# Cross-attention on one core: the energies by three float32r passes over halves of gx and y in place of Strassen's seven float32 products, and the values made with positions on the partitions

## The chip, the cores and the metric

The kernel runs on one core of a Trainium2 chip. The metric is the device time of one launch in microseconds, taken from runs of the whole program; the profile is one further look at one execution, with the start and the end of every instruction on TensorE (its weight loads as a row of their own, PEld), VectorE (DVE), ScalarE (ACT), GpSimd (POOL) and SyncE (SP).

## The reference

There are 32 batches; in each, `x` and the context `y` have 256 channels and 1024 positions, in float32. What is computed for a batch:

```python
x_q = einsum('oc,bcn->bno', w_qk, y)
x_k = einsum('oc,bcn->bon', w_qk, x)
x_v = einsum('oc,bcn->bon', w_v, x) + b_v
energy = einsum('bnc,bcm->bnm', x_q, x_k)          # 1024 x 1024
attention = softmax(energy, axis=-1)
attention = attention / (1e-07 + attention.sum(axis=1, keepdims=True))
x_r = einsum('bcn,bnm->bcm', x_v, attention)
out = x + relu(einsum('oc,bcn->bon', w_t, x - x_r) + b_t)
```

The kernel folds the weights once: gx is x under w_qk's own product (with the sign turned), so that an energy is y times gx over 256 channels; "values" are x under the product of w_t and w_v (with the sign turned), so that the attention product gives the output's channels at once.

## The kernel before

Everything is float32. A 256 x 1024 operand is seen as four quadrants of 128 partitions x 512 columns, and each of the four products of a batch (gx, values, energies, attention) is made by Strassen's scheme in the form with seven products (class `Seven`, line 252): products p1, p5, p2, p6, p3, p7, p4, of which several are added onto one another in the same PSUM bank, and four combinations c11, c12, c22, c21. The scheme keeps three banks: p6 is added onto p1's bank, ScalarE then copies that bank to SBUF (`kept`, tag `w`), and only then p7 and p4 may be added onto it; c11 reads p2's bank and the copy of p1. A product takes factors that are sums of quadrants: for x these (`xs`) are made by accumulating DMAs on GpSimd's queue (lines 225 to 250), for y (`ys`) in the same way, for gx (`gt`, line 324) and the values (`us`, line 384) by four GpSimd operations of 512 columns each.

For each batch b, in the loop at line 664:

- **Energies** (class `Energy`, lines 402 to 455). For each of four steps t, seven products of 128 x 512 give the four quadrants of two rows of tiles (rows t and t + 4, each 128 x 1024). ScalarE evicts three partial sums; VectorE combines each quadrant with one custom instruction that also keeps the running minimum (or, for the rows t + 4, the maximum) and is followed by a small read of that accumulator (`nm`). ScalarE takes the exponential of a row of 1024 (`exp`) and its sum (`rs`), VectorE takes the reciprocal (`ri`) and adds the scaled row to `acc` (`share`); one row in eight is scaled by ScalarE. The combination c21 reads a constant tile `zeros`.
- After the first step t = 0, the last product of the batch before (`before.end()`, five products) and its combination c21 with the store are made.
- **gx of batch b + 1** (class `Keys`), then most of the **values of b + 1** (class `Values`). The values come out with channels on the partitions and are needed with positions on the partitions: `turn` (line 367) makes four VectorE transposes of 32 x 32 blocks, and `move` (line 375) sixteen copies of 32 partitions x 512, split between VectorE (8 a batch) and ScalarE (8 a batch), or DMAs in the first and the last batch. The bias of the values is added on ScalarE.
- `columns` and `inverse` (lines 597 and 611) sum `acc` over the partitions and take the reciprocals `rc`.
- **Attention** (class `Attention`, lines 457 to 595). `normal` scales the rows of `e` by both reciprocals (16 VectorE operations of 512), `mix` makes the sums of their quadrants (eight of 1024, tiles `et` for t1, t2 and t4), and each of the seven products is five TensorE products: one of x (`xpart`) and four over tiles of `e` (`epart`). The results are combined with relu and x and stored.

Every compute engine's instructions run in the order in which the program issues them: the class `InOrder` (line 66) chains each instruction of TensorE, VectorE, ScalarE and GpSimd to the one before it on the same engine:

```python
behind = nullcontext() if self.last is None else tc.issue_after(self.last.ins)
with behind:
    self.last = getattr(self.engine, name)(*args, **kwargs)
```

So an instruction that waits holds up all that stands behind it on its engine. SyncE's DMAs are placed by the framework. All matrix results use one pool of eight PSUM banks of 512 columns, taken in rotation (line 64); evictions and combinations go through a pool of two buffers a tag (`temp`, line 219). All TensorE, VectorE, ScalarE and GpSimd instructions carry line 77 in the profile, since `InOrder` issues them; they are told apart by their tiles: `pg` gx, `pu` values, `pe` energies, `po` attention.

Of the kernel before, what the change touches and what calls it, by code (L numbers as in the profile page):

```python
# [9 lines left out]
F32 = mybir.dt.float32  # L10
AF = mybir.ActivationFunctionType
ALU = mybir.AluOpType
# [4 lines left out]
def kernel(  # L17
# [22 lines left out]

# [12 lines left out]
    BIG = 3.0e38  # L59

    const = ctx.enter_context(tc.tile_pool(name="const", bufs=1))
    xp = ctx.enter_context(tc.tile_pool(name="xp", bufs=2))
    yp = ctx.enter_context(tc.tile_pool(name="yp", bufs=1))
# [25 lines left out]
    def load(tag, b, pieces=1):  # L89
        from_, p = (x, xp) if tag == "x" else (y, yp)  # L90
        to = p.tile([P, KC, N], F32, tag=tag, name=f"{tag}_{b}")
        from_ = from_[b].rearrange("(k p) n -> p k n", p=P)
        W = KC // pieces
        for j in range(pieces):
            nc.sync.dma_start(to[:, ts(j, W)], from_[:, ts(j, W)])
        loaded[tag, b] = to
# [18 lines left out]
    scratch = ep.tile([P, 3, HT, MB], F32, tag="et", name="scratch").rearrange(  # L115
# [8 lines left out]
    bv = scratch[:, 4, :KC].rearrange("p (k o) -> p k o", o=1)  # L124
    bt = const.tile([P, KC, 1], F32, name="bt")
    nbt = const.tile([P, KC, 1], F32, name="nbt")
    bu = const.tile([P, KC, 1], F32, name="bu")
    nbu = const.tile([P, KC, 1], F32, name="nbu")
    for k, start in enumerate((nc.sync.dma_start, act.dma_start)):
        start(wqk[:, k], w_qk[ts(k, P)])  # L130
    load("x", 0, KC)
# [4 lines left out]
    load("y", 0)  # L136


    zeros = const.tile([P, MB], F32, name="zeros")
    few = const.tile([P, P], F32, name="few")  # L140
    dve.memset(few, 0.0)
    dve.memset(zeros, 0.0)
# [35 lines left out]
    _, g_left = lefts("g", pg, -1.0)  # L178
# [19 lines left out]
    def value_bias(wtT):  # L198

        pb = bank("pb")  # L200
        for i in range(KC):
            for k in range(KC):
                pe.matmul(
                    pb[:, i : i + 1],
                    wtT[:, k, ts(i, P)],
                    bv[:, k, :],
                    start=(k == 0),
                    stop=(k == KC - 1),
                )
        act.mul(nbu[:, :, 0], pb[:, :KC], 1.0)  # L210
        act.mul(bu[:, :, 0], pb[:, :KC], -1.0)
        act.mul(nbt[:, :, 0], bt[:, :, 0], -1.0)
# [12 lines left out]
    def summed(tag, b):  # L225


        p = up if tag == "x" else one
        s = p.tile([P, 4, MB], F32, tag=f"{tag}s", name=f"{tag}s_{b}")
        t1, t3, t4, t2 = (s[:, j] for j in range(4))  # L230
        to = loaded[tag, b]
# [8 lines left out]
        else:  # L240
            from_ = (x if tag == "x" else y)[b]
            q = quarters(from_)
# [3 lines left out]
                lambda: accumulate(s[:, :2], corners(from_)),  # L246
# [3 lines left out]
        return (b11, b21, b22, t4, t1, t2, t3), steps  # L250

# [52 lines left out]
    class Keys(Seven):  # L304


        def __init__(self, b, xr):
            super().__init__("g", b)
            self.xr = xr
            self.gx = one.tile([P, KC, N], F32, tag="gx", name=f"gx_{b}")  # L310
# [4 lines left out]
        def block(self, i, h):  # L315
            return self.gx[:, i, ts(h, MB)]

        def combine(self, i, h, in0, in1, op):
            dve.tensor_tensor(self.block(i, h), in0, in1, op)

        def c21(self):
            act.copy(self.block(1, 0), self.one)

        def factors(self):


            a11, a12, a21, a22 = (self.block(i, h) for h, i in ((0, 0), (0, 1), (1, 0), (1, 1)))
            gt = one.tile([P, 4, MB], F32, tag="gt", name=f"gt_{self.b}")
            s1, s2, s3, s4 = (gt[:, j] for j in range(4))
            pool.tensor_tensor(s1, a21, a22, ALU.subtract)  # L330
            pool.tensor_tensor(s2, s1, a11, ALU.subtract)
            steps = [
                lambda: pool.tensor_tensor(s4, s2, a12, ALU.add),
                lambda: pool.tensor_tensor(s3, a11, a21, ALU.subtract),
            ]
            return (a11, a12, s4, a22, s1, s2, s3), steps

    class Values(Seven):
# [8 lines left out]
        def product(self, into, j, onto=False):  # L347
            matmul(into, u_left[j - 1], self.xr[j - 1], onto)

        def bias(self, tag):  # L350
            return {"p1s": bu[:, 0, :], "w": nbu[:, 0, :], "p5s": bu[:, 1, :]}[tag]

        def kept(self, p, tag):
            s = temp(tag, f"u{tag}_{self.b}")
            act.activation(s, p, AF.Identity, bias=self.bias(tag), scale=1.0)
            return s
# [7 lines left out]
        def c21(self):  # L364
            act.activation(self.block(1, 0), self.one, AF.Identity, bias=bu[:, 1, :], scale=1.0)

        def turn(self):

            self.turned = one.tile([P, KC * MH, MB], F32, tag="turned", name=f"turned_{self.b}")
            for i in range(KC):  # L370
                for h in range(MH):
                    dve.transpose(self.turned[:, i * MH + h], self.block(i, h))
            self.moves = [(a, g) for a in range(NG) for g in range(NG)]

        def move(self, count, by):

            from_ = self.turned.rearrange("p b (k c) -> p (b k) c", c=G32)
            to = self.ut.rearrange("p i h (k c) -> p (i h k) c", c=G32)
            from_, to = (v.rearrange("p (k g) c -> p k g c", g=NG) for v in (from_, to))
            for a, g in self.moves[:count]:  # L380
                by(to[ts(g, G32), :, a, :], from_[ts(a, G32), :, g, :])
            self.moves = self.moves[count:]

        def factors(self):

            us = up.tile([P, 4, MB], F32, tag="us", name=f"us_{self.b}")
# [13 lines left out]
    class Energy(Seven):  # L400
# [3 lines left out]
        def __init__(self, b, t, lhs, rhs):  # L404
            super().__init__("e", f"{b}_{t}")
            self.t = t
            self.lhs, self.rhs = lhs, rhs
            self.ends = {}

        def product(self, into, j, onto=False):  # L410
            matmul(into, self.rhs[j - 1][:, ts(self.t, P)], self.lhs[j - 1], onto)

        def combine(self, i, h, in0, in1, op):


            n = h * HT + self.t
            nm = sp.tile([P, 1], F32, tag=f"nm{i}", name=f"nm_{self.b}_{h}_{i}")
            dve.tensor_tensor_reduce(
                out=e[:, n, ts(i, MB)],
                in0=in0 if h == 0 else in1,  # L420
                in1=in1 if h == 0 else in0,
                scale=1.0,
                scalar=self.ends.get(h, BIG if h == 0 else -BIG),
                op0=op,
                op1=ALU.min if h == 0 else ALU.max,
                accum_out=nm,
            )
            if (i, h) == (1, 1):
                bias = sp.tile([P, 1], F32, tag="bias", name=f"bias_{self.b}")
                dve.tensor_scalar(bias, nm, -1.0, None, ALU.mult)  # L430
                nm = bias
            self.ends[h] = nm

        def c21(self):
            self.combine(1, 0, self.one, zeros, ALU.add)

        def exp(self, h):
            n = h * HT + self.t
            rs = sp.tile([P, 1], F32, tag="rs", name=f"rs_{self.b}_{h}")
            act.activation(  # L440
                e[:, n, :], e[:, n, :], AF.Exp, bias=self.ends[h], scale=2.0 * h - 1.0, accum_out=rs
            )
            self.rs = rs

        def scale(self, h):
            n = h * HT + self.t
            ri = sp.tile([P, 1], F32, tag=f"ri{n}", name=f"ri_{self.b}_{h}")
            dve.reciprocal(ri, self.rs)
            scales[n] = ri

        def share(self, h):

            n = h * HT + self.t
            self.scale(h)
            dve.scalar_tensor_tensor(acc, e[:, n, :], scales[n], acc, ALU.mult, ALU.add)

    class Attention(Seven):


        def __init__(self, b, xr, ur):  # L460
# [3 lines left out]
            et = ep.tile([P, 3, HT, MB], F32, tag="et", name=f"et_{b}")  # L464
            self.b11, self.b12 = e[:, :HT, ts(0, MB)], e[:, :HT, ts(1, MB)]
            self.b21, self.b22 = e[:, HT:, ts(0, MB)], e[:, HT:, ts(1, MB)]
            self.t1, self.t2, self.t4 = (et[:, j] for j in range(3))
            self.t3 = self.t1
# [45 lines left out]
        def put(self):  # L514

            i, h, z = self.left.pop(0)
            xt = loaded["x", self.b]
# [3 lines left out]
        def c21(self):  # L521
            z = temp("z", f"z_{self.b}_1_0")
            act.activation(z, self.one, AF.Relu, bias=bt[:, 1, :], scale=1.0)
            dve.tensor_tensor(z, z, loaded["x", self.b][:, 1, ts(0, MB)], ALU.add)
# [9 lines left out]
        def run(self, u, before=None):  # L534
# [35 lines left out]
            if u:  # L570
                self.epart(self.two, 3, (3,))
                self.c12()
                u.turn()
# [5 lines left out]
        def finish(self):  # L579

            xb = temp("op1s", f"xb_{self.b}")
            act.activation(
                xb, loaded["x", self.b][:, 1, ts(0, MB)], AF.Identity, bias=bt[:, 1, :], scale=1.0
# [44 lines left out]
    load("x", 1)  # L628
    xr, _ = summed("x", 0)
# [4 lines left out]
    g.c11()  # L634
# [3 lines left out]
    g.c12()  # L638
    g.p7()
    g.c22()  # L640
    u_left = value_weights(wtT)
    value_bias(wtT)
    g.p4()
    g.c21()
    rhs, _ = summed("y", 0)
    lhs, gsteps = g.factors()
    for step in gsteps:
        step()
    gsteps = []
    xn, xsteps = summed("x", 1)  # L650
# [13 lines left out]
    for b in range(B):  # L664
        more = b + 1 < B
        pair = []

        for t in range(HT):
            now = Energy(b, t, lhs, rhs)
# [176 lines left out]
```

## Time and profile before

| what | us |
|---|---|
| three runs: lowest, median, highest | 2134.31, 2134.49, 2134.91 |
| the profiled execution: span from its first to its last instruction | 2132.3 |
| what of the runs' median lies outside such a span | 2.2 |
| TensorE busy | 2126.5 (100%) |
| VectorE busy | 1903.7 (89%) |
| ScalarE busy | 946.4 (44%) |
| GpSimd busy | 550.4 (26%) |
| energy products (`pe` rows, together) | 915.0 |
| transposes `turned<-ut` on VectorE, 128 | 79.4 |
| moves `ut<-turned` on VectorE, 246, and on ScalarE, 247 | 102.5 and 151.9 |

The profile has no time of its own for the profiled execution beyond its span; the table's third row is the difference of the two rows above it. A line of the timeline gives the start, the duration, the engine, the line, the operation, its output and inputs with their shapes, and how many such instructions follow one another; in brackets stands the idle time ahead of it and what ended it. A float32 product shows as two TensorE records. Durations of products overlap their successors', so that what a product costs is read from start to start.

### The profile page before, as it was taken

What the parts mean: (1) busy time and instruction counts of PE and PEld (TensorE: products, weight loads), DVE (VectorE), ACT (ScalarE), POOL (GpSimd) and SP (SyncE); (2) the same over time, 40 slices, a digit from 0 to 9 for tenths busy, and PEclk for the clock granted to TensorE, in tenths of its full rate; (3) what the DMA queues carried; (4) which work ended last, traced back from release to release, by engine and by line L of the source; (5) the groups of instructions that cost most, each with busy time, mean ns of one, the idle gap of its engine ahead of it and who ended that gap; (6) DMA issues with size and microseconds to landing.
All of it is one profiled execution on the core that took longest, in us unless ns stands there. A gap on an engine that the chain in (4) does not pass through costs nothing.

```text
span 2132.3 us, 17692 instructions
## 1 busy us (share of the span) xinstructions
PE 2126.5 (100%) x4966; PEld 939.7 (44%) x4966; DVE 1903.7 (89%) x3493; ACT 946.4 (44%) x1570; POOL 550.4 (26%) x489
## 2 busy tenths in 40 slices
PE   9999999999999999999999999999999999999999
PEld 4444444444444444444444444444444444444443
DVE  6899888998888988889888898888998889988898
ACT  5334554335543355433454334543345434455342
POOL 4322323222222122221222212223123232232320
PEclk9999999999999999999999999999999999999999
DMA  6444544445444454443544445544455544454440
GB/s 169 104 110 112 138 129 104 119 103 138 128 109 124 93 140 127 110 128 91 140 127 116 122 97 130 133 122 110 109 121 131 135 104 107 118 133 134 104 92 30
DMA packets 115810, 250.14 MB, mean 117 GB/s; under 512 B 18688, under 2 KB 19456, under 8 KB 115712
## 3 DMA queue, kind: packets, MB, share of 16 engines
q1 hardware_dynamic: 72912, 167.60, 23.3%
q0 software_dynamic: 42656, 81.28, 23.3%
q8 instruction: 40, 0.66, 0.1%
q14 instruction: 58, 0.48, 0.1%
q10 hardware_dynamic: 144, 0.13, 0.0%
HBM read 181.67 MB, written 33.55 MB: 101 GB/s over the span
## 4 chain that ended last, share of the span: by engine, by line
PE 98%; DVE 1%; DMA 0%; issue 0%; POOL 0%; SPq 0%; DVEq 0%; POOLq 0%
PE po L77 44%; PE pe L77 36%; PE pu L77 9%; PE pg L77 9%; DVE e L77 1%; DMA x<-in_x_dram 0%; DVE acc L77 0%; DVE et L77 0%; DVE parts L77 0%; PE pw L77 0%; POOL xs L77 0%; DVE rc L77 0%; DVE sc L77 0%; PE pb L77 0%; DVE z L77 0%
## 5 line engine op out<-in xcount | busy, mean ns | idle before, releaser
L77 PE MATMUL pe<-gt,ys 128*128 128x512 f32 x768 | 392.1, 592 | 0.0
L77 DVE SCALAR_TENSOR_TENSOR e<-e,ri,rc 128x512 f32<-128x512 f32 x512 | 347.3, 745 | 1.1
L77 PE MATMUL po<-et,us 128*128 128x512 f32 x768 | 347.2, 594 | 0.1
L77 DVE SCALAR_TENSOR_TENSOR acc<-e,ri,acc 128x1024 f32<-128x1024 f32 x224 | 287.8, 1285 | 8.1
L77 PE MATMUL pe<-gx,y 128*128 128x512 f32 x512 | 261.4, 592 | 0.0
L77 PEld LDWEIGHTS pe<-gt,ys 128*128 128x128 f32 x768 | 145.8, 190 | 184.0 <-issue 181.7
L77 PEld LDWEIGHTS po<-et,us 128*128 128x128 f32 x768 | 143.3, 190 | 188.4 <-issue 146.4
L77 PE MATMUL po<-e,ut 128*128 128x512 f32 x512 | 224.9, 592 | 0.0
L77 ACT COPY ut<-turned 32x512 f32<-32x512 f32 x247 | 151.9, 615 | 157.9 <-DVE turned L77 155.0
L77 ACT ACTIVATE e<-e,nm 128x1024 f32<-128x1024 f32 x128 | 147.1, 1149 | 98.0 <-DVE nm L77 96.5
L77 POOL TENSOR_TENSOR gt<-gx 128x512 f32<-128x512 f32 x64 | 80.8, 1263 | 379.6 <-DVE gx L77 379.6
L77 DVE TENSOR_TENSOR et<-e 128x1024 f32<-128x1024 f32 x128 | 153.7, 1221 | 2.3
L77 PEld LDWEIGHTS po<-e,ut 128*128 128x128 f32 x512 | 97.3, 190 | 122.5 <-issue 99.0
L77 PEld LDWEIGHTS pe<-gx,y 128*128 128x128 f32 x512 | 97.3, 190 | 122.5 <-issue 122.0
L77 ACT ACTIVATE e<-e,bias 128x1024 f32<-128x1024 f32 x128 | 147.4, 1152 | 0.7 <-DVE bias L77 0.5
L77 DVE CUSTOM_DVE_ANT_0 e<-pe,ep1s 128x512 f32<-128x512 f32 x128 | 88.5, 691 | 63.2 <-ACT e L77 61.4
L77 POOL TENSOR_TENSOR us<-ut 128x512 f32<-128x512 f32 x64 | 81.6, 1276 | 202.0 <-ACT ut L77 192.6
L77 PE MATMUL pe<-gx,ys 128*128 128x512 f32 x256 | 130.8, 592 | 0.2 <-DVE nm L77 0.2
L77 PE MATMUL pe<-gt,y 128*128 128x512 f32 x256 | 130.7, 592 | 0.0
L77 ACT COPY ep1s<-pe 128x512 f32<-128x512 f32 x128 | 74.5, 582 | 110.7 <-PE pe L77 106.4
L77 PE MATMUL po<-e,us 128*128 128x512 f32 x256 | 120.5, 592 | 0.0
L77 DVE CUSTOM_DVE_ANT_0 e<-pe,zeros,nm 128x512 f32<-128x512 f32 x128 | 95.7, 747 | 26.9 <-PE pe L77 25.7
(121 smaller groups left out, 3194.8 us busy)
## 6 DMA issues: line engine op xcount, KB each, us to landing
y<-in_ctx_dram SPq DMA_DIRECT2D x32, 1024.0 KB, 4.8
out_dram<-z SPq DMA_DIRECT2D x128, 256.0 KB, 2.1
x<-in_x_dram SPq DMA_DIRECT2D x31, 1024.0 KB, 5.8
xs<-in_x_dram SPq DMA_DIRECT2D x62, 512.0 KB, 4.5
ys<-in_ctx_dram SPq DMA_DIRECT2D x62, 512.0 KB, 4.6
xs<-in_x_dram POOLq DMA_DIRECT2D x31, 512.0 KB, 6.2
xs<-xs POOLq DMA_DIRECT2D x31, 512.0 KB, 5.0
ys<-in_ctx_dram POOLq DMA_DIRECT2D x31, 512.0 KB, 6.2
```

Of the source, the lines that this page charges most:

```text
L77: self.last = getattr(self.engine, name)(*args, **kwargs)
```

## The change

- **Energies.** Strassen's scheme for the energies goes, with `gt`, `ys`, `zeros` and the maximum for the lower rows. For gx and for y three float32r forms are made of every quadrant (`forms`): a high half, a low half, and a difference of the two at scales 4096 apart, on ScalarE (two multiplies) and GpSimd (two subtractions). The quadrant itself stands in a small buffer of 512 columns (tag `c`, two buffers), into which y is loaded by DMA in four pieces and gx is combined. A row of tiles is then, for each of two halves of 512 columns, six float32r products in two banks: two forms' products of two 128-channel parts in the first bank, and the third form's in the second (`products`). ScalarE evicts the first bank with a factor, VectorE adds the second and keeps the minimum (`gather`). Rows are made one after the other, 0 to 7; `exp` follows one row behind, `share` two rows behind; the first share of a batch is a scale on VectorE.
- **Values.** The operands of the value products change places: x is the stationary side, in four slices of 128 positions, and the folded weights are the moving side, with 128 columns. The results have positions on the partitions, so `turn` and `move` go. The bias becomes a tile of 128 columns for each part, added by two GpSimd operations of 1024 columns at the start of `factors`.
- **Order.** The multiplies of `forms` stand on ScalarE's queue where gx is combined: `forms(0, 0)` between p5's copy and p6's copy of gx, `forms(0, 1)` and `forms(1, 1)` ahead of the value products' copies, `forms(1, 0)` after c21; those of y stand in the attention. `us` and `et` shrink (one buffer in place of two; two parts in place of three, t4 in place of t2).

The core of the diff:

```diff
     class Keys(Seven):
...
+        def forms(self, i, h):
+            c = self.chunks.pop((i, h))
+            high, low, both = (self.gf[:, j, i, ts(h, MB)] for j in range(3))
+            part = cp.tile([P, MB], F32R, tag="h", name=f"gh_{self.b}_{i}_{h}")
+            act.mul(high, c, UNDER / UP)
+            act.mul(part, c, UNDER)
+            pool.tensor_tensor(low, c, value(part), ALU.subtract)
+            pool.tensor_tensor(both, value(high), value(low), ALU.subtract)
...
     class Values(Seven):
         def product(self, into, j, onto=False):
-            matmul(into, u_left[j - 1], self.xr[j - 1], onto)
+            for t in range(HT):
+                pe.matmul(
+                    into[:, ts(t, P)],
+                    self.xr[j - 1][:, ts(t, P)],
+                    u_left[j - 1],
+                    start=(t == 0 and not onto),
+                    stop=(t == HT - 1),
+                    skip_group_check=True,
+                )
...
-        def turn(self):
...
-        def move(self, count, by):
...
         def factors(self):
-            us = up.tile([P, 4, MB], F32, tag="us", name=f"us_{self.b}")
+            us = one.tile([P, 4, MB], F32, tag="us", name=f"us_{self.b}")
+            for i in range(KC):
+                tiles = self.ut[:, i].rearrange("p h (t c) -> p (h t) c", c=P)
+                pool.tensor_tensor(tiles, tiles, bu[:, i : i + 1].to_broadcast([P, NT, P]), ALU.add)
...
-    class Energy(Seven):
+    class Energy:
...
+        def products(self, h):
+            self.sums = [bank(f"pe{j}_{self.b}_{self.n}_{h}") for j in range(2)]
+            for j in range(3):
+                for k in range(KC):
+                    pe.matmul(
+                        self.sums[j // 2],
+                        self.yf[:, j, k, ts(self.n, P)],
+                        self.gf[:, j, k, ts(h, MB)],
+                        start=(k == 0 and j != 1),
+                        stop=(k == KC - 1 and j != 0),
+                    )
+
+        def gather(self, h):
+            s = temp(("p1s", "p5s")[h], f"es_{self.b}_{self.n}_{h}")
+            act.mul(s, self.sums[0], OVER)
+            nm = sp.tile([P, 1], F32, tag=f"nm{h}", name=f"nm_{self.b}_{self.n}_{h}")
+            dve.tensor_tensor_reduce(
+                out=e[:, self.n, ts(h, MB)], in0=self.sums[1], in1=s,
+                scale=1.0, scalar=self.low, op0=ALU.add, op1=ALU.min, accum_out=nm,
+            )
+            self.low = nm
...
-        for t in range(HT):
-            now = Energy(b, t, lhs, rhs)
...
+        for n in range(NT):
+            now = Energy(b, n, q.yf, g.gf)
+            rows.append(now)
+            now.products(0)
...
+            now.gather(0)
+            now.products(1)
+            now.gather(1)
+            if n == 0:
...
+                    before.end()
+                    before.c21()
+                    load(b + 1)
...
+            if n > 0:
+                rows[n - 1].exp()
+            if n > 1:
+                rows[n - 2].share()
...
         if more:
+            q = Queries(b + 1)
             g = Keys(b + 1, xn)
             g.p1()
-        last.exp(1)
...
+            rows[-1].exp()
+            rows[-2].share()
             g.p5()
+            g.p2()
+            g.c11()
+            g.forms(0, 0)
+            rows[-1].share()
+            g.p6()
+            columns(b)
+            g.p3()
+            g.c12()
+            g.forms(0, 1)
             g.p7()
-            g.c12()
             g.c22()
+            g.forms(1, 1)
             un = Values(b + 1, xn)
             un.p1()
             un.p5()
             un.p2()
             un.p6()
```

The forms of y (class `Queries`) are made in the same way as those of gx, from the loaded pieces.

## The prediction on record

> **What bounds the kernel now.** I read the page's first part, then a batch of the timeline on TensorE, then the row of energies on VectorE.
>
> ```profile
> PE 2126.5 (100%) x4966; PEld 939.7 (44%) x4966; DVE 1903.7 (89%) x3493; ACT 946.4 (44%) x1570; POOL 550.4 (26%) x489
> ```
>
> TensorE is never idle; VectorE, at 89%, is close behind. Two starts of the same product, one batch apart, in TensorE's timeline:
>
> ```profile
> 640.49 1.02 PE L77 MATMUL pg<-x,g 128*128 128x512 f32 x2
> ...
> 645.64 1.02 PE L77 MATMUL pg<-xs,gs 128*128 128x512 f32 x2
> 646.50 1.02 PE L77 MATMUL pu<-x,wvtT 128*128 128x512 f32 x2
> ...
> 706.63 1.02 PE L77 MATMUL pg<-x,g 128*128 128x512 f32 x2
> ```
>
> A batch takes 66.14 us. A float32 product of 512 columns is two records and costs 0.86 us, start to start (645.64 to 646.50; 0.859 over many). A batch has 28 of them for energies, 7 for gx, 7 for values, 35 for the attention: 77 x 0.859 = 66.1. So only TensorE's sum counts today. VectorE in the energies:
>
> ```profile
> 633.37 0.75 DVE L77 CUSTOM_DVE_ANT_0 e<-pe,zeros,nm 128x512 f32<-128x512 f32 x1
> 634.04 0.08 DVE L77 DVE_READ_ACCUMULATOR2_ANT nm<- 128x1 f32 x1
> 634.04 0.68 DVE L77 CUSTOM_DVE_ANT_0 e<-ew,pe 128x512 f32<-128x512 f32 x1
> 634.65 0.08 DVE L77 DVE_READ_ACCUMULATOR2_ANT nm<- 128x1 f32 x1
> 634.88 0.75 DVE L77 CUSTOM_DVE_ANT_0 e<-pe,ep5s,nm 128x512 f32<-128x512 f32 x1
> 635.55 0.08 DVE L77 DVE_READ_ACCUMULATOR2_ANT nm<- 128x1 f32 x1
> 635.67 0.15 DVE L77 TENSOR_SCALAR bias<-nm 128x1 f32<-128x1 f32 x1
> 635.74 0.15 DVE L77 RECIPROCAL ri<-rs 128x1 f32<-128x1 f32 x1
> 635.93 1.29 DVE L77 SCALAR_TENSOR_TENSOR acc<-e,ri,acc 128x1024 f32<-128x1024 f32 x1
> ```
>
> A gather holds the queue 0.61 us, one that needs the minimum just read waits 0.23 first and holds it 0.67, a reciprocal takes 0.20, a share 1.20 (632.17 to 633.37).
>
> **TensorE's sum after.** Energies become 8 rows x 2 halves x 6 = 96 float32r passes of 512 columns. Before has none. Bounds: 0.101 us, the pace of eight records that load 128 weights for one column (last line below), to 0.429, one record of a float32 product. I take 0.215: a product of two float32 numbers in halves is four half products in two records, and float32r operands that are already halves need one, half a record. Energies: 96 x 0.215 = 20.6, for 24.05. The Trainium skill (FP8 and Floating Point Precision, TensorE Precision Notes) says that true FP32 is four passes and a reduced form truncates; a quarter of 0.859 is 0.215 too, but the page gives no rate for float32r, and the 0.429 stays possible.
>
> The value products become 28 float32 products of 128 columns, 56 records.
>
> ```profile
> 10.32:10.76 0.44, 0.44 (x5) 0.43 (x4) 0.00 (x0) 0.24 (x1) 0.44 (x2) 1.00 0.97 391
> 12.48:14.21 1.73, 1.73 (x10) 1.52 (x9) 1.48 (x3) 0.38 (x1) 0.04 (x1) 1.00 1.02 414
> 14.21:15.02 0.81, 0.81 (x10) 0.81 (x8) 0.20 (x1) 0.38 (x1) 0.81 (x1) 1.00 1.04 412
> ```
>
> In these stretches (first column its time, then busy TensorE and weight loads) four 128-column transposes take 0.44 us, eight 256-column records 1.73 (0.216 each), eight one-column records 0.81. So 128 columns cost 0.107 of streaming, and the load, 0.101, lies beside it: 0.11 each, 6.16 us for 6.01. Bounds: 0.107 to 0.208 where load and stream don't overlap. TensorE's sum is 66.14 - 3.45 + 0.15 = 62.85, a gain of 3.3 us a batch if nothing else becomes late. It becomes late.
>
> **VectorE.** Gone: 4 transposes (0.62 each), 8 moves (0.43), 4 biases: 6.3 us a batch; but they stand at the end of the attention, where VectorE then waits for the product `end` anyway. The 16 gathers and 8 shares stay, in 20.6 us for 24. A row costs VectorE 0.61 + 0.23 + 0.67 + 0.20 + 1.20 = 2.91 us, TensorE 12 x 0.215 = 2.58. Today the order of the quadrants hides most of these reads; after, the second gather always follows its own minimum.
>
> A batch with time 0 at energy row 0:
> - Row 0 to 2.58, `end` (five products) to 6.87, row 1 to 9.45 and 0.1 for a bank: row 2 at 9.55. VectorE waits for `end` with c21's add, so it goes into row 2 without backlog.
> - Row 2's first gather: four passes 0.86, 0.20 to ScalarE (21.29 + 0.859 to 22.35), its scaled eviction 0.6, 0.1: 11.3. The second half is ready at 12.6; gather and reciprocal to 13.45; share 0 is a one-input scale of 1024, bounds 0.83 (two COPYs of 512, 0.417) to 1.20 (the share): 0.85, as it has one tensor input like the COPY. 14.3.
> - Rows 3 to 7: 5 x 2.91 to 28.9. Share 6, 1.4: 30.3. Then only gx's first quadrant (c11), though its product ended at 27.6.
> - ScalarE's order after is gp1s, exp, gp5s, **the two multiplies on c11's quadrant, then gw**. The copy gw (0.58) is what gx's seventh product waits for, since it adds to the bank that gw reads. c11 0.68, 0.1, two multiplies 0.55 each, gw 0.58, 0.15 with a weight load laid bare: the seventh product starts at 32.9. TensorE is ready at 25.0 + 5 x 0.859 = 29.2. It stands **3.7 us**, more than the whole gain.
> - It ends at 33.8, three value products (0.88 each) at 36.4. The sixth waits for the copy up1s, behind four more multiplies: c12 ends at 34.1, c22 at 34.75, the multiplies at 36.4, the copy at 37.0: 37.1, another 0.7.
> - From there VectorE has caught up (normals start at 37.9, TensorE's use of them at 43.2): 0.88 + 0.88 + 0.86 + 0.88 + 2.58 + 24.07 (27 products and one of values) = 30.15, to 67.25.
>
> So a batch takes 67.3, **1.15 more**. ScalarE's 16 evictions, 16 multiplies and 8 exponentials are some 2.4 us a row, under 2.91. An ACTIVATE without a bias tensor has no 512 row: 0.38 (256 wide) to 0.69 (with bias); 0.6 follows the nearer.
>
> GpSimd gets 16 subtractions of 512 (1.27 each, 20.3 us) and two adds of 1024 (bounds 1.27 and 2.53; 2.5 as four of 512 take four times one), and loses four for gt and three DMAs for y: half a batch, beneath the rest. Two places are near: c22 needs the buffer of c11's quadrant, free at 33.5 against 34.1 (if that cover is gone, c22 and the sixth value product slip with it); and the last y forms for row 0 end at 65.4 against 67.3. The chain for xs starts after the us adds, at 10.4, and its three DMAs (5.2 apart) land by 27, ahead of 27.6 where the sixth product needs the second. On SP's queue four y loads of 256 KB replace 1 MB and two of 512 KB; they wait for chunk buffers, arrive by 51, and hold stores that are not due. x's load starts 16 us ahead of its use and landed in 5.8. All cost nothing.
>
> **Start and tail.** Before the first energy GpSimd has 4 sums and, from 16.5 on, 14 subtractions: row 0 at 34.6 for 21.3. TensorE stands idle for 7 us ahead of it, and may start as slowly as at the beginning, where ten 128-column records took 0.235 us each (1.06 to 3.41) for the later 0.11: 1.4. Together 14.7 later. Bounds: nothing (the values' products fill it) and 18. In the last batch VectorE's normals start at 31.5 after row 0 rather than 33.97: 2.5 gained.
>
> Sum: 31 x 1.15 + 14.7 - 2.5 = 47.9. The profiled span is 2132.3; the three runs lie at 2134.31 to 2134.91, so some 2.2 us lie outside. 2134.5 + 47.9 = **2182**.
>
> A rule that speaks against more: the Trainium skill (TensorE: Matmul & The Clock Gate, Part 1) says that some 3.4 us of an idle array halves the clock until 3.4 us of work. Here the granted clock falls only once, to 0.67 in the last 2.3 us, which have no matmul at all; the stall falls into 1.0 and 2.5 us. If each did trip it, 1.7 us a batch would be added: 2235.
>
> **Rivals.**
> - *VectorE is not late (faster).* It decides at c11: 30.3 has to become 28.7 or less to break even (1.15 and the start's share, 0.4, a batch). That is a row of 2.6 us for 2.91. Without any delay a batch is 62.9: 2134.5 - 31 x 3.3 + 12 = 2044; with half of it gone, about 2105. For it: VectorE loses 6.3 us of work, and 0.101 a pass instead of 0.215 would start row 2 some 2.7 earlier. Against: the rows above hold the same instructions back to back.
> - *A float32r pass costs a full record*, 0.429: energies 41.2 us, VectorE keeps up, but the gw chain still costs some 2: 85 us a batch, about 2740. For: no row shows less for 512 columns.
> - *Weight loads laid bare* in the 128-column products, 0.208: 56 x 0.1 = 5.5 a batch, 2350. Against: the windows above.
> - *The change doesn't do what it says*: the program has no transposes or moves left and the 96 passes are there, so no chance is set apart.
>
> **How the numbers follow.** The chain as above, 2150 to 2225: 0.60. VectorE less late: 0.20, of which 0.07 under 2095. Between the two, no change: 0.05. Weight loads bare, in part or whole: 0.10, of which 0.06 over 2250. Full record: 0.05. Range 2095 to 2250, which leaves 0.18 out. This kernel's measurement tells 0.2%, about 4 us, from no change. Faster 0.20, same 0.05, slower 0.75.
>
> **What would show it.** Right: TensorE's busy share falls to 93 or 94%; in each batch it waits for ScalarE's gw some 2 to 3.5 us ahead of pg's seventh product; c11 starts right after a share; pe passes 0.21 to 0.22 apart; VectorE busy without gaps from row 2 to the normals. Wrong: pg's seventh product without a wait, passes 0.43 apart, pu's 128-column records over 0.13 apart, or waits on POOL's forms.

## The result and the profile after

The changed kernel takes 2401.22 us (median of four runs, 2385.16 to 2416.03); before takes 2134.64 beside it: a ratio of 1.125 (95% interval 1.118 to 1.131). The four runs lie at two levels, near 2386 (mean granted clock 0.968) and near 2416 (0.949); why was not tried, and all that follows of this kernel is read from the profiled run, at 2385.16, of the lower level. Its span is 2383.2 us, 250.9 more than that of before. The forecast was 2182, the range 2095 to 2250: the direction was right, but the kernel became 266.6 us slower where 47.9 were forecast, more than five times as much.

The page of the changed kernel: engines, chain by engine, and three groups (busy us, mean ns of one, then idle time before them and what ended it).

```profile
PE 2170.7 (91%) x7586; PEld 1322.8 (56%) x7586; DVE 2014.7 (85%) x3024; ACT 1085.4 (46%) x1930; POOL 1217.8 (51%) x838
...
PE 57%; DVE 33%; issue 3%; POOL 3%; ACT 2%; DVEq 0%; DMA 0%; ACTq 0%; POOLq 0%
...
L73 DVE SCALAR_TENSOR_TENSOR e<-e,ri,rc 128x512 f32<-128x512 f32 x512 | 580.0, 1197 | 1.1
L73 PE MATMUL po<-et,us 128*128 128x512 f32 x768 | 379.1, 636 | 88.1 <-DVE et L73 88.1
...
L73 PE MATMUL pg<-xs,gs 128*128 128x512 f32 x192 | 112.8, 672 | 68.8 <-ACT gw L73 67.4
```

TensorE is no longer the whole chain: a third of it is VectorE. Two waits are new. One is the wait for the copy gw, which was forecast: 67.4 us, 31 times 2.2. The other, 88.1 us for VectorE's sums `et` in the attention, was not. And the 512 normals (the scalings of `e` by `normal`), the same instruction with the same tiles as before, take 1197 ns each. Their row in the page of before:

```profile
L77 DVE SCALAR_TENSOR_TENSOR e<-e,ri,rc 128x512 f32<-128x512 f32 x512 | 347.3, 745 | 1.1
```

Where this happens is seen in one batch. The timelines of VectorE, then of GpSimd, in the changed kernel (start, length, in us):

```profile
668.09 14.82 DVE L73 SCALAR_TENSOR_TENSOR e<-e,ri,rc 128x512 f32<-128x512 f32 x10
682.95 1.22 DVE L73 TENSOR_TENSOR et<-e 128x1024 f32<-128x1024 f32 x1
684.09 1.41 DVE L73 SCALAR_TENSOR_TENSOR e<-e,ri,rc 128x512 f32<-128x512 f32 x2
```

```profile
668.22 1.75 POOL L73 TENSOR_TENSOR gf<-gx,gh 128x512 fp32r<-128x512 f32 x1
670.04 1.61 POOL L73 TENSOR_TENSOR gf<-gf 128x512 fp32r<-128x512 f32 x1
...
674.96 1.72 POOL L73 TENSOR_TENSOR yf<-y,yf 128x512 fp32r<-128x512 f32 x1
...
680.11 1.60 POOL L73 TENSOR_TENSOR yf<-yf,yh 128x512 fp32r<-128x512 f32 x1
```

The first ten normals of a batch of before, for comparison:

```profile
652.99 6.71 DVE L77 SCALAR_TENSOR_TENSOR e<-e,ri,rc 128x512 f32<-128x512 f32 x10
```

Ten normals take 14.82 us in place of 6.71, while GpSimd makes eight subtractions from 668.22 to 681.71. Both engines suffer: a subtraction that takes 1.27 us alone takes 1.59 to 1.75 here (one takes 1.36). Each pair of a normal and a subtraction fills some 1.7 us (13.49 / 8), not much less than the two after one another (0.67 + 1.27 = 1.94). As soon as GpSimd is done, two normals take 1.41 us again, the old pace.

What TensorE does meanwhile (the wait stands in brackets; gp5s and gw are ScalarE's copies of gx's products, up1s one of the values'):

```profile
659.54 1.12 PE L73 MATMUL pg<-x,gs 128*128 128x512 f32 x2 [0.28 <-ACT gp5s L73]
662.84 1.12 PE L73 MATMUL pg<-xs,gs 128*128 128x512 f32 x2 [2.17 <-ACT gw L73]
...
667.12 1.16 PE L73 MATMUL pu<-wvtTs,xs 128*128 128x128 f32 x8 [0.48 <-ACT up1s L73]
...
673.33 5.31 PE L73 MATMUL po<-e,ut 128*128 128x512 f32 x12
678.96 1.13 PE L73 MATMUL po<-e,ut 128*128 128x512 f32 x2 [0.31 <-DVE e L73]
680.63 1.12 PE L73 MATMUL po<-e,ut 128*128 128x512 f32 x2 [0.55 <-DVE e L73]
684.32 5.37 PE L73 MATMUL po<-et,us 128*128 128x512 f32 x8 [2.56 <-DVE et L73]
689.52 1.02 PE L73 MATMUL po<-xs,wtTs 128*128 128x512 f32 x2
```

Up to the first product with `e`, at 673.33, the prediction's ledger (its list of a batch's times) holds: with its time 0 at 629.5, where the products ahead of energy row 0 end, it put that product at 672.7. From 673.33 on twelve products at its 0.859 end at 683.6, but the next one starts at 689.52. The waits 0.31, 0.55 and 2.56 are 3.4 of these 5.9 us; the eight records at 684.32 take 5.37 us where eight of the same kind take 3.6 elsewhere (the granted clock is 0.5 from 684.80 to 688.21, see below).

**The sum.** From the second batch to the last, the starts of a batch's first gx product lie 73.5 us apart on average (66.14 before): 30 x 7.33 = 219.9 us. The first batch starts its own 20.5 later, and the last stretch is 10.4 longer: 250.8 of the 250.9.

### The profile page after: what moved, and what is told of

It reads as the page before. It is cut to its first block, busy times and chain, and to the rows that moved or that the text cites. A ratio compares the mean times of both kernels' runs of the same rounds, so it can differ in the third digit from the quotient of the medians.

```text
span 2383.2 us, 23847 instructions
## 1 busy us (share of the span) xinstructions
PE 2170.7 (91%) x7586; PEld 1322.8 (56%) x7586; DVE 2014.7 (85%) x3024; ACT 1085.4 (46%) x1930; POOL 1217.8 (51%) x838
## 3 DMA queue, kind: packets, MB, share of 16 engines
q0 software_dynamic: 21328, 40.64, 10.6%
## 4 chain that ended last, share of the span: by engine, by line
PE 57%; DVE 33%; issue 3%; POOL 3%; ACT 2%; DVEq 0%; DMA 0%; ACTq 0%; POOLq 0%
PE pe L73 28%; PE po L73 28%; DVE e L73 22%; DVE et L73 3%; POOL gf L73 3%; DVE gx L73 2%; DVE acc L73 2%; DVE rc L73 2%; DVE sc L73 1%; PE pu L73 1%; DVE parts L73 1%; ACT gf L73 1%; ACT es L73 1%; ACT gh L73 1%; DVE ri L73 0%
## 5 line engine op out<-in xcount | busy, mean ns | idle before, releaser
L73 PE MATMUL pe<-gf,yf 128*128 128x512 f32 x3072 | 735.2, 398 | 2.8 <-POOL yf L73 1.6
L73 PEld LDWEIGHTS pe<-gf,yf 128*128 128x128 f32 x3072 | 576.3, 188 | 151.3 <-issue 29.2
L73 DVE SCALAR_TENSOR_TENSOR e<-e,ri,rc 128x512 f32<-128x512 f32 x512 | 580.0, 1197 | 1.1
L73 PE MATMUL po<-et,us 128*128 128x512 f32 x768 | 379.1, 636 | 88.1 <-DVE et L73 88.1
L73 POOL TENSOR_TENSOR yf<-y,yf 128x512 fp32r<-128x512 f32 x128 | 200.0, 1563 | 493.8 <-ACT yf L73 493.8
L73 ACT ACTIVATE es<-pe 128x512 f32<-128x512 f32 x512 | 304.4, 595 | 284.8 <-PE pe L73 284.1
L73 POOL TENSOR_TENSOR gf<-gx,gh 128x512 fp32r<-128x512 f32 x128 | 176.6, 1380 | 300.2 <-ACT gh L73 288.5
L73 DVE SCALAR_TENSOR_TENSOR acc<-e,ri,acc 128x1024 f32<-128x1024 f32 x224 | 289.8, 1294 | 8.0
L73 DVE CUSTOM_DVE_ANT_0 e<-pe,es,nm 128x512 f32<-128x512 f32 x256 | 192.4, 751 | 72.0 <-ACT es L73 47.1
L73 POOL TENSOR_TENSOR yf<-yf,yh 128x512 fp32r<-128x512 f32 x128 | 200.9, 1570 | 10.0
L73 DVE CUSTOM_DVE_ANT_0 e<-pe,es 128x512 f32<-128x512 f32 x256 | 175.2, 685 | 34.1 <-ACT es L73 30.2
L73 POOL TENSOR_TENSOR gf<-gf 128x512 fp32r<-128x512 f32 x128 | 182.9, 1429 | 10.2
L73 PE MATMUL pg<-xs,gs 128*128 128x512 f32 x192 | 112.8, 672 | 68.8 <-ACT gw L73 67.4
```

## The experiments

**Theory A**: VectorE's instructions with two SBUF inputs (normals, `et`) and GpSimd's subtractions, which read SBUF, hold one another up; a second, smaller loss is the wait for gw, because ScalarE's multiplies stand ahead of that copy. **Rivals**: B, GpSimd's mere being busy or something else in the new layout slows the normals; C, only the wait for gw matters, and the rest follows from it; D, the values' part of the change costs the time.

### x1_writes_only: GpSimd as busy, but reading nothing for the forms

Both `forms` of after, gx's and y's:

```diff
-            pool.tensor_tensor(low, c, value(high), ALU.subtract)
-            pool.tensor_tensor(both, value(low), value(part), ALU.subtract)
+            for form in (low, low, low, both, both, both):
+                pool.memset(value(form), 1.0)
```

> The kernel after, with each of GpSimd's two subtractions of a quadrant's forms replaced by three memsets of the same tile, so that GpSimd is about as busy but reads nothing from SBUF; the low and the third forms are left out of the computation. Theory A (a VectorE instruction with both inputs in SBUF waits while a GpSimd instruction reads SBUF): the normals, 1.20 us each in the changed kernel, come back to 0.75, the first ten take 6.7 us for 14.8, and a batch falls from 73.4 to about 67.9: 2230 us, 2200 to 2260. Rival B (VectorE is slowed by ScalarE's or TensorE's traffic, or by any busy GpSimd): the normals stay near 1.2 and the time at 2385 to 2416.

Measured: 2237.04 us, 1.046 times before (1.043 to 1.049). Groups of its page:

```profile
L73 DVE SCALAR_TENSOR_TENSOR e<-e,ri,rc 128x512 f32<-128x512 f32 x512 | 347.4, 746 | 1.1
L73 PE MATMUL po<-et,us 128*128 128x512 f32 x768 | 345.6, 592 | 0.8 <-DVE et L73 0.8
...
L73 PE MATMUL pg<-xs,gs 128*128 128x512 f32 x192 | 122.2, 723 | 70.1 <-ACT gw L73 68.6 <-ACT gp1s L73 1.6
```

One batch, on VectorE and on GpSimd:

```profile
1802.86 6.71 DVE L73 SCALAR_TENSOR_TENSOR e<-e,ri,rc 128x512 f32<-128x512 f32 x10
```

```profile
1802.70 13.11 POOL L73 MEMSET yf<- 128x512 f32 x24
```

GpSimd is as busy as in after (1228 us for 1218), and its memsets run beside the normals, which are back at 746 ns. The waits for `et` are gone and those for gw stay. So rival B falls: what hurts is that GpSimd reads. With what follows from it, that is worth 2401 - 2237 = 164 us of the 267.

### x2_before_reads: the same collision put into the kernel before

```diff
+    def spare(count):
+        for _ in range(count):
+            pool.tensor_tensor(junk, rc[:, :MB], zeros, ALU.subtract)
...
+            spare(3)
+            ysteps[1]()
+            spare(2)
+            ysteps[2]()
+            spare(5)
...
-            ysteps[1]()
-            ysteps[2]()
```

> The kernel before, with ten GpSimd subtractions of 512 columns of spare data added to each batch, placed from the start of the normals between GpSimd's DMAs, and nothing else. Theory A: five of them fall into the normals and the first sums, where VectorE has no slack against TensorE, and cost about 1 us each; five later ones partly: 5 to 7 us a batch, 2290 to 2350 us, with TensorE waiting for e and et. Rival B: the added work lies beside the rest, 2134 to 2142.

Measured: 2543.13 us, 1.191 times before (1.189 to 1.194). One batch, on VectorE and on GpSimd:

```profile
846.44 16.04 DVE L77 SCALAR_TENSOR_TENSOR e<-e,ri,rc 128x512 f32<-128x512 f32 x10
862.52 2.17 DVE L77 TENSOR_TENSOR et<-e 128x1024 f32<-128x1024 f32 x1
864.61 3.42 DVE L77 SCALAR_TENSOR_TENSOR e<-e,ri,rc 128x512 f32<-128x512 f32 x2
```

```profile
846.75 5.08 POOL L77 TENSOR_TENSOR junk<-rc,zeros 128x512 f32<-128x512 f32 x3
...
858.68 8.80 POOL L77 TENSOR_TENSOR junk<-rc,zeros 128x512 f32<-128x512 f32 x5
```

With nothing else changed but the place of two DMA issues, ten subtractions that nobody uses slow the normals beside them as in the changed kernel (1.67 us from start to start in both; two of the ten here took 2.5 and 2.8), and `et` too (2.17 for 1.22). The mechanism is the one expected; the size was missed by 190 us or more. A batch became 12 to 15 us longer, not 5 to 7: all ten subtractions fell on instructions with two SBUF inputs, and the batches show 3.4 to 13.7 us at half clock.

### x3_copy_first: gw and the values' copies ahead of the multiplies

On ScalarE, `forms(0, 0)` moves behind p6's copy (gw), and `forms(0, 1)` and `forms(1, 1)` behind p6's copy of the values:

```diff
-            g.forms(0, 0)
             g.p6()
+            g.forms(0, 0)
...
-            g.forms(0, 1)
...
-            g.forms(1, 1)
             un.p6()
+            g.forms(0, 1)
+            g.forms(1, 1)
```

(Context and the lines between are shortened.)

> The kernel after, with the order on ScalarE alone changed: the copy gw and the copies of the value products stand ahead of the multiplies of gx's forms. Theory A: VectorE's chain from energy row 2 through the normals to the sum t1 sets the batch, so the waits for gw (2.2 us), gp5s and up1s go, and TensorE waits as much longer for the normals and t1: 2385 to 2416, within 15 us of the kernel after. Rival C (the gw wait, which the prediction priced, is on the path): 2.6 us a batch less, about 2320.

Measured: 2439.66 us, 1.143 times before (1.142 to 1.145), more than the changed kernel itself. What TensorE waited for (us in total, times, longest):

```profile
PE po L73 <- DVE et L73: 111.3, 33, 3.6
PE po L73 <- DVE e L73: 93.0, 187, 1.0
```

The wait for gw is gone from this list and the batch is 74.8 to 75.4 us all the same. gx's forms, made later, bring more of GpSimd's subtractions onto the normals (310 of the 512 lie beside one, for 271, and the mean is 1294 ns for 1197), and TensorE, which comes to the attention earlier, waits there for longer. This refutes C: taking away the only wait that the prediction had found makes the kernel slower. It is 24 us above the band that theory A gave; the extra subtractions on the normals had been left out of it.

### x4_both: both edits

> The edits of the first and the third kernel of this set together; the low and the third forms are left out of the computation. Theory A: with the contention gone, the gw chain is on the path, and taking it away too leaves TensorE's sum, 64.4 us a batch, and some 0.6 for a late t1: about 65, 2120 us, 2095 to 2150, so 2.6 us a batch under the first kernel. Rival B: as the kernel after. If the gw chain costs nothing even then, the time is that of the first kernel.

The edits of x1 and x3 together; like x1, it measures time alone, since the low and third forms are constants. Measured: 2113.94 us, 0.990 times before (0.989 to 0.992). One of its batches in the windows (first to last moment and length; busy PE, PEld, DVE, ACT and POOL; granted clock; share of DMA; GB/s):

```profile
1751.30:1816.10 64.80, 64.52 (x237) 40.03 (x236) 55.62 (x95) 33.78 (x60) 38.54 (x59) 1.00 0.33 86
```

TensorE is busy but for 0.28 us: this batch is what the float32r passes are worth without the two losses. The changed kernel loses 8.7 us (73.5 - 64.8) a batch to both.

### x5_fill_the_wait: x1 with work in the wait

```diff
+            un.one = un.bank(1)
+            for _ in range(FILL):        # FILL = 10
+                pe.matmul(un.one[:, :P], few, few, start=True, stop=True)
             g.p7()
```

(`un`, the values' object, is made ahead of them, and its first product then overwrites the bank that they use.)

> x1_writes_only (GpSimd only writes; low and the third form are constants) with ten 128-column products of constants put on TensorE ahead of the seventh gx product, where x1 waits 2.2 us for gw. They take 10 * 0.11 = 1.1 us, so the wait falls to 1.1 us and no work moves. First theory: of the 4.0 us a batch between x1 and x4, some 2.5 us is the wait itself and the rest is the half clock that the wait brings; with a wait of 1.1 us the clock stays at 1.0, the batch is about 67.4 us and the time 2195 us (2180 to 2215). Rival: the half clock has another cause, or costs nothing: the time stays that of x1, 2237 (2225 to 2250), or more by the products.

Measured: 2207.15 us, 1.034 times before (1.033 to 1.036), 30 us less than x1 though TensorE does more. The wait, in x1 and then in x5:

```profile
1796.94 2.08 PE L73 MATMUL pg<-xs,gs 128*128 128x512 f32 x2 [2.52 <-ACT gw L73]
1798.81 1.91 PE L73 MATMUL pu<-wvtT,x 128*128 128x128 f32 x8
```

```profile
1698.05 2.39 PE L74 MATMUL pu<-few 128*128 128x128 f32 x20
1700.45 1.12 PE L74 MATMUL pg<-xs,gs 128*128 128x512 f32 x2
1701.41 1.05 PE L74 MATMUL pu<-wvtT,x 128*128 128x128 f32 x8
```

One term of the expectation was wrong: a float32 product is two records, so the ten cover 2.4 us, all of the wait, and not 1.1. For the question this is as good: seventh product and batch stand where they stood, and only the clock differs. Behind the bare wait eight records take 1.91 us, behind the filled one 1.05. The windows of three batches of x1 and one of x5 (columns as above):

```profile
1720.50:1789.20 68.70, 66.19 (x237) 41.02 (x236) 55.85 (x95) 33.88 (x60) 38.27 (x58) 0.98 0.31 81
1789.20:1859.50 70.30, 67.51 (x238) 42.32 (x237) 55.87 (x95) 33.89 (x60) 37.91 (x58) 0.95 0.31 79
2065.70:2133.60 67.90, 64.98 (x238) 40.15 (x237) 55.77 (x95) 33.67 (x60) 38.36 (x59) 1.00 0.33 82
```

```profile
1693.00:1760.90 67.90, 67.20 (x258) 42.54 (x257) 55.76 (x95) 33.71 (x60) 38.10 (x58) 1.00 0.31 82
```

With a wait of 2.23 us, x1's batches take 67.9 us at a clock of 1.00 and 68.7 at 0.98; the one at 0.95, with 2.52, takes 70.3 (others at 0.95, with 2.23, take 70.1). Nearly all of x5's take 67.9. So the fall of the clock costs x1 (2237.04 - 2207.15) / 31 = 1.0 us a batch, and the wait with what goes along with it the other 3.0 of the 4.0 that part x1 and x4.

### x6_values_only: the other half of the change by itself

Before with `turn` and `move` taken out, the value products with x as the stationary side, and the bias added by GpSimd; the energies are those of before. Its core:

```diff
-            matmul(into, u_left[j - 1], self.xr[j - 1], onto)
+            for t in range(HT):
+                pe.matmul(into[:, ts(t, P)], self.xr[j - 1][:, ts(t, P)], u_left[j - 1], ...)
...
-                u.turn()
...
+                pool.tensor_tensor(tiles, tiles, bu[:, i : i + 1].to_broadcast([P, NT, P]), ALU.add)
```

> The kernel before with one part of the change alone: the values are made with positions on the partitions, the 32x32 turns and the moves of blocks between partitions go, and the bias is added by GpSimd in two additions a batch; the energies stay as they were (Strassen, float32). Taken from the engines a batch: some 6.3 us of VectorE and 4.7 us of ScalarE; given to GpSimd: two additions of some 2.6 us; TensorE: 6.16 for 6.01 us. First theory: the turns lay beside TensorE's work, so 31 * 0.15 = +5 us: 2140 us (2132 to 2150). Rival 1: VectorE at 89 per cent was late somewhere in the batch and taking work from it shortens the batch: below 2128. Rival 2: GpSimd's additions read SBUF and stop VectorE's instructions with two SBUF inputs where they fall together, or add a wait: above 2150.

Measured: 2146.2 us, 1.0055 times before (1.0038 to 1.0072). A batch takes 66.34 us for 66.14, and the first energy comes 4.6 us later: 30 x 0.2 + 4.6 = 10.6 of the 11.9 us. So D falls, with 12 us of the 267, and the turns on VectorE had been free. One group of its page shows the collision again, off the path:

```profile
L77 DVE SCALAR_TENSOR_TENSOR z<-z,x 128x512 f32<-128x512 f32 x96 | 154.1, 1629 | 1.2
```

These instructions took 686 ns in before; GpSimd's additions now lie beside 61 of the 96. TensorE wants nothing of them then, and the batch grew by no more than the 0.2 us.

### v2_two_halves: the change built along theory A

Two forms in place of three, so one subtraction for each quadrant, and an order in which most subtractions wait for the first t sum:

```diff
+        def high(self, i, h):
+            act.mul(self.f[:, 0, i, ts(h, MB)], self.chunks[i, h], 1.0)
+        def low(self, i, h):
+            c = self.chunks.pop((i, h))
+            high, low = (self.f[:, j, i, ts(h, MB)] for j in range(2))
+            pool.tensor_tensor(low, c, value(high), ALU.subtract)
...
+            for at, (p, q_) in enumerate(((0, 0), (0, 1), (1, 0))):
...
+            def late(t1):
+                pool.tensor_copy(behind, t1[:, HT - 1, :1])
+                g.low(1, 0)
+                for at in corners_:
+                    q.low(*at)
```

> The changed kernel rebuilt along the first theory (VectorE's instructions with two SBUF inputs stand still beside GpSimd's subtractions; ScalarE's multiplies stand ahead of gw). The three energy passes are high*high, high*low and low*high, summed in one PSUM bank; the product of the two low halves, some 2^-24 of the whole, is left out. So each form needs one ScalarE multiply and one GpSimd subtraction instead of two and two (8 subtractions a batch for 16), and the eviction of the first bank by ScalarE goes. y is loaded earlier, gw and the copies of un are put ahead of the multiplies, and the subtractions of the last gx form and of all four y forms wait for the first t sum of the attention, so they lie behind the ten normals. First theory: normals back at 0.75 us, no wait for gw over 0.5 us, 64.5 to 65 us a batch, some 4 us more at the start: 2095 us (2085 to 2125), faster than before. Rival: the normals were slow through something else in the change (the values' new layout, y's loads): they stay above 1 us and the batch at 70 or more: 2260 or more. Between the two, if the late subtractions now hold up the mixes that follow the normals: up to 4 us a batch, 2200.

Measured: 2236.5 us, 1.048 times before (1.047 to 1.050): the case between the two, and 36 us above its 2200. One batch on VectorE and on GpSimd:

```profile
626.73 6.72 DVE L71 SCALAR_TENSOR_TENSOR e<-e,ri,rc 128x512 f32<-128x512 f32 x10
...
637.80 6.52 DVE L71 SCALAR_TENSOR_TENSOR e<-e,ri,rc 128x512 f32<-128x512 f32 x4
644.25 3.41 DVE L71 TENSOR_TENSOR et<-et,e 128x1024 f32<-128x1024 f32 x2
```

```profile
637.35 0.18 POOL L71 COPY behind<-et 128x1 f32<-128x1 f32 x1 [11.10 <-DVE et L71]
637.49 1.27 POOL L71 TENSOR_TENSOR gf<-gx,gf 128x512 fp32r<-128x512 f32 x1
638.72 6.73 POOL L71 TENSOR_TENSOR yf<-y,yf 128x512 fp32r<-128x512 f32 x4
```

The collision only moved. The ten normals are free of it, but four normals and the second t sum stand behind the gate; four normals take 6.52 us (2.73 in after), and TensorE waits 2.93 us for `et` in every batch but the first.

### v3_behind_t4: the subtractions behind the last sum

```diff
             self.mix(self.t4, self.b21, self.t2, ALU.subtract)
+            if late:
+                late(self.t4)
```

(The call of `late` behind t1 goes.)

> v2_two_halves with one edit: GpSimd's five late subtractions (the last gx form, the four y forms) wait for the fourth t sum (t4) instead of the first. In v2 they began at t1, in the middle of the twelfth to sixteenth normals and the second t sum, and TensorE stood 2.9 us a batch for that sum; ahead of the gate the ten normals were back at 6.72 us. Behind t4 VectorE stands idle for 3.5 us in v2 and then has sums with one operand in PSUM. The five take 5 * 1.27 = 6.4 us; energy row 0 begins 3.9 us after t4 and wants the gx form in its third and fourth pass, so it may wait up to 0.5 us. First theory: no wait of TensorE above 0.6 us, no half clock, 64.5 to 65.2 us a batch: 2236 - 31 * 3.8 = 2118 us (2105 to 2135), a little faster than before. Rival: row 0 waits for the late forms and the clock falls with it, 2 us a batch or more: 2165 or more.

Measured: 2124.62 us (2119.73 to 2125.37), 0.995 times before (0.993 to 0.996). The engines of its page, then one batch on VectorE and on GpSimd:

```profile
PE 2078.9 (98%) x7586; PEld 1291.8 (61%) x7586; DVE 1774.5 (84%) x3025; ACT 692.0 (33%) x1162; POOL 801.8 (38%) x613
```

```profile
615.93 0.68 DVE L71 TENSOR_TENSOR z<-po,ow 128x512 f32<-128x512 f32 x1
619.28 0.69 DVE L71 TENSOR_TENSOR z<-op5s,po 128x512 f32<-128x512 f32 x1 [2.66 <-PE po L71]
619.88 3.54 DVE L71 SCALAR_TENSOR_TENSOR z<-z,x 128x512 f32<-128x512 f32 x2
```

```profile
616.22 1.27 POOL L71 TENSOR_TENSOR gf<-gx,gf 128x512 fp32r<-128x512 f32 x1
617.44 5.44 POOL L71 TENSOR_TENSOR yf<-y,yf 128x512 fp32r<-128x512 f32 x4
```

GpSimd's reads now lie beside VectorE's idle 2.66 us, sums with one operand in PSUM, and two `z` that nobody on TensorE wants soon (3.54 us for some 1.4). Most batches take 64.9 us at a clock of 1.00. With the product of the two low halves left out, this is faster than both kernels: 0.5% under before, 11.5% under the changed one.

## Why the prediction was wrong, point by point

- **The step that failed** is the paragraph on GpSimd: "half a batch, beneath the rest", ended by "All cost nothing", and with it "From there VectorE has caught up": it put the cost of the subtractions to VectorE at nothing. They were counted (16, at 1.27 us) and checked for their due times, and nobody asked what runs beside them. Beside them ran the normals: 0.67 us became 1.68, start to start, VectorE's lead of 5.3 us at the attention (37.9 against 43.2) became a wait, and the attention lost 5.9 us. x1 shows the cause (reads, not busyness), x2 shows it without the change. The trace of before held a hint: no normal stood beside a computation of GpSimd there, but 30 of the 31 additions of one form of `z` did and took 0.98 to 0.99 us; the 31st, beside none, took 0.684, like the other form. The rows of before that should have been read are these two groups:

```profile
L77 DVE SCALAR_TENSOR_TENSOR z<-z,x 128x512 f32<-128x512 f32 x96 | 63.4, 686 | 1.2
...
L77 DVE TENSOR_TENSOR z<-z,x 128x512 f32<-128x512 f32 x31 | 30.2, 975 | 44.8 <-ACT z L77 44.8
```

- The Trainium skill (SBUF — State Buffer, Who interferes with whom) says that a VectorE instruction with two SBUF inputs contends with a GpSimd instruction that reads SBUF, not with one that only writes it, and that an instruction with at most one SBUF input does not (outside VectorE's 2-port modes). The runs agree: 746 ns beside memsets, 1.75 us beside subtractions, and the energies' custom gathers, with one operand in PSUM, at 685 and 751 ns in before and after alike, though in after 175 of the 512 lie beside a computation of GpSimd. The page also calls the shared ports an exclusive lock; that one side stands still for all of the other's instruction is not quite what the pairs show, with 1.68 us for 0.67 and 1.27. The page was not weighed in the prediction.
- **The wait for gw** was right: seventh product at 33.3 after the ledger's time 0 (32.9 forecast), up1s after it. TensorE stood 2.4 us there, not 3.7, because its own rows were slower and it came later.
- **A float32r pass** is 0.227 us start to start, inside a row and from bank to bank (0.215 taken). Energies: 96 x 0.227 = 21.8 us for 20.6, and TensorE's sum is 66.14 - 24.05 + 21.8 + 0.2 = 64.1, not 62.85. So the gain to be had was some 2.0 us a batch, not 3.3; x4, whose batch shown takes 64.8, got 1.3 of them.
- **The value products** cost what was said (0.11 a record), and x6 shows +0.2 us a batch for the +0.15 and that VectorE's turns had been hidden.
- **The clock** was priced but left out of the sum, since a stall of 1.0 and 2.5 us was short of the rule: that was wrong. The skill's rule (TensorE: Matmul & The Clock Gate, Part 1), as the prediction told it, needs some 3.4 us idle; here waits of 2.2 to 2.5 us were followed by half clock in 28 of 30 batches of x1, and, after the first batch, in none of x5, where the wait was filled. It costs 1.0 us a batch in x1; the prediction's price, if it tripped, was 1.7.
- **The start**: 20.5 us later for 14.7. The first energy came at 40.9 us after 21.3; the idle time ahead of it (8.7 us for up1s, 5.7 for gx) also brought 13.7 us at half clock.
- **The rivals**: "VectorE is not late" named the right engine but the wrong place; none of them had VectorE's own instructions getting longer, so the prediction held no price for the loss that came. All durations were taken from before as if an instruction had one price.

So the batch: 66.14 + 1.15 was forecast. The first product with `e` came 0.6 later than in the ledger, and the attention added 5.9: 73.8, and the batch shown, from 655.67 to 729.42, took 73.75. The direction was not luck: without the collision (x1) the kernel still takes 2237.04 us, 102 more than before, with the wait for gw that was forecast.

## What to carry to other kernels

A duration read from a trace holds for the neighbours that the instruction had there. Before moving work to an idle GpSimd, list what VectorE does in that stretch: if those are instructions with both inputs in SBUF and TensorE waits for them, the work isn't free, however idle GpSimd is. Put it beside instructions that read PSUM, or behind the last result that somebody waits for: moving the same subtractions from behind t1 to behind t4 saved 3.6 us a batch (v2 and v3: 2236.5 and 2124.62 us).

## What was not expected of the hardware

- The collision lengthens both sides: 0.67 to 1.68 us, start to start, for a normal, 1.27 to 1.6 or 1.75 for a subtraction, a pair in 1.68 us where the two alone make 1.94; writes by GpSimd (0.525 us memsets, back to back) leave VectorE at 746 ns.
- The granted clock falls to half for 3.4 or 6.8 us after a wait of TensorE of no more than 2.2 to 2.5 us, though not after every one (x1: batches of 67.9, 68.7 and 70.1 us with the same wait of 2.23). The trace of x1 shows what parts them: every stretch at half clock begins on one grid of 3.41 us, and, from its second batch to the middle of its last, the clock fell behind all 28 steps of that grid in which TensorE stood idle for 1.76 us or more, and behind none with less (two had 1.75 and 1.69). So where the wait falls on the grid decides; this is read from the trace, and no run moved a wait along the grid. Work without a use in that wait made the kernel 30 us faster.
- float32r: 0.227 us for 128 x 512, a quarter of a float32 product's 0.859 and 6% over it.
